# Layer 1 of a four-layer graph network: all turned parts of the factors prepared ahead of the loop, in the first product buffer of the round

## The chip, the cores and the metric

The kernel runs on one core of one Trainium2 chip. The metric is the device time of one execution in microseconds; for the kernel before, three executions took 556.18, 557.09 and 557.86 us, so the median is 557.09 us. The engines are named as in the profile: PE (TensorE), with PEld for its weight loads, DVE (VectorE), ACT (ScalarE), POOL (GpSimd) and SP (SyncE, which here issues DMAs).

## The reference

Four layers run one after the other on a graph of 3327 nodes with 64 features each and a dense matrix `adj` of 3327 x 3327. Each is `x = layernorm(x + layer(x, adj))`. The change lies in layer 1, a hyperbolic attention layer:

```python
x_tan = _logmap0(x, C)
left = x_tan @ att_W[:D] + att_b
right = x_tan @ att_W[D:]
adj_att = jax.nn.sigmoid(left + right.T) * adj
x_local = _logmap(x[:, None, :], x[None, :, :], C)
support_t = jnp.einsum('ij,ijd->id', adj_att, x_local)
return _proj(_expmap(x, support_t, C), C)
```

For every pair of nodes i and j a logarithmic map is needed, whose only part that belongs to the pair is a function of the product of the two nodes' vectors. All the rest splits into factors that belong to i alone or to j alone.

## The kernel before

The nodes are padded to 26 blocks of 128. Two blocks, number b and number b + 13, stand side by side in one tile of 128 partitions, 64 features each, so that a turned matrix (features in partitions, nodes in columns) has 13 blocks of 128 columns. `riT` is the turned factor of the nodes i; `ljT[0]` is that of the nodes j; `ljT[1]` is the same with its two halves of partitions exchanged. Where a part of `ljT[0]` is made, two DMAs from the one to the other tile, issued by SP (`change_over`), make the same part of `ljT[1]`.

The loop of layer 1 goes over 104 tiles. A tile t is one block j (128 rows) against 832 of the columns i: two pieces of 416, one in each half. Two tiles that follow each other share the block j and make a pair. For each tile there are these steps:

- `attention` (once a pair): ACT computes `sg`, the sigmoid, 1664 columns; POOL multiplies it by the adjacency `at`. SP loads `at` into one of four buffers (`load`, line 1058); the last four blocks are kept in SBUF (`kept`).
- `products`: PE makes `pq`, the products of the vectors, in PSUM (line 1103; each of the two matmuls of float32 counts as more than one instruction in the profile).
- `linear`: DVE makes `a` from `pq` and `sg` (line 1115), and then ACT squares `pq` in place (line 1116).
- `gather`: DVE makes `v` from the squared `pq` and `a` (line 1124), and PE multiplies it into the accumulator `acc` (line 1136).

A pass (`cp`) over all 26 blocks makes 52 tiles, with two accumulators; there are two passes. In the first pass ACT also makes the rows `xv` of a block to come, one for each pair (`rows_of_sums`, line 1230).

The products stand in three PSUM buffers of two banks each, from the pool `n1q`; a buffer is used again when its last reader is done, which for a product is `v`. [...] Ahead of the loop the same six banks belong to another pool, `n1p`, in which the first parts of the factors are made.

PE, ACT, DVE and POOL carry out their instructions in the order in which the code writes them (a manual schedule); only SP's order is left to the scheduler. So the order of the calls is the order of the engines. In the loop it is, for each t: `linear(t + 1)`, then `gather(t)`, which after `v` calls `products(t + 3)`, then the attention of a pair to come.

The factors are turned on PE, by transposes against `ident` into PSUM; a copy then brings them to SBUF. Only a part of it is done before the loop: `right` of blocks 9 to 12 and 5 to 8 (the latter called `seventh`), `turn` of blocks 0 to 7. Four parts are made in the loop (`later`): at t = 13 `right` of blocks 1 to 4 and `turn` of 8 to 11, at t = 25 `right` of block 0 and `turn` of 12. At these two tiles `prepare` takes a product buffer (`prep_t` in the profile) for the transposes, ACT copies them out (line 1214) in the next step, and `products(t + 3)` is called behind the gather instead of ahead of it:

```python
if extra:
    copies.extend(prepare(f"t{t}", extra))
if not extra:
    products(t + 3)
```

`by_rows` is a further part, the factor `lf` turned to 26 rows, made in the bank of the second accumulator; `spread_left` later stores it to DRAM and loads it back, spread over all partitions.

Of the kernel before, what the change touches and what calls it, by code (L numbers as in the profile page):

```python
# [10 lines left out]
F32 = mybir.dt.float32  # L11
# [8 lines left out]
P = 128  # L20
N = 3327
NB = 26
# [54 lines left out]
def kernel(  # L77
# [819 lines left out]
    with tc.tile_pool(name="l1", bufs=1) as l1:  # L897
# [20 lines left out]
        with tc.tile_pool(name="l1a", bufs=1) as l1a, tc.tile_pool(  # L918
            name="l1ap", bufs=1, space=PSUM
        ) as l1ap:  # L920
            v = l1a.tile([P, NB], F32, name="v")
            sums = l1a.tile([P, NB], F32, name="sums")
# [88 lines left out]
        def near_sphere(mT, ljT_0, xm, sq_e, t_e, rows_63):  # L1011
# [3 lines left out]
            with tc.tile_pool(name="n1", bufs=1, reuse_waits="tile") as n1, tc.tile_pool(  # L1015
# [45 lines left out]

                orders = (order, sorted(order, key=lambda jb: jb in kept))
                tiles = [(cp, jb, ci) for cp in range(2) for jb in orders[cp] for ci in range(2)]
                us, pqs, a_s, accs, copies, sums = {}, {}, {}, {}, [], []

                def attention(pair):

# [49 lines left out]
                        pqs[t], pqs[t], AF.Square, bias=al[:, one], scale=ga[:, one]  # L1117
                    )

                def gather(t, extra=()):  # L1120

                    cp, jb, ci = tiles[t]
                    w = n1w.tile(TW, F32, tag="v", name=f"v_{t}")
                    stt(w, pqs.pop(t), CUBIC_REST, a_s.pop(t), op0=ALU.add, op1=ALU.mult)  # L1124
                    while sums:
                        sums.pop(0)()
                    if extra:
                        copies.extend(prepare(f"t{t}", extra))
                    if not extra:
                        products(t + 3)  # L1130
                    if jb == orders[cp][0]:
                        accs[cp, ci] = n1c.tile(
                            [P, CW], F32, tag=f"acc{ci}", name=f"acc1_{cp}_{ci}"
                        )
                    for h in range(2):
                        nc.tensor.matmul(  # L1136
                            accs[cp, ci][h * D : (h + 1) * D, :], xv[:, slot(jb), :], w[:, h, :],
                            start=(jb == orders[cp][0]), stop=(jb == orders[cp][-1]),
                        )
                    if extra:  # L1140
                        products(t + 3)
                    if jb == orders[cp][-1]:
                        of = slice((2 * cp + ci) * CW, (2 * cp + ci + 1) * CW)
                        sums.append(lambda: nc.scalar.copy(mT[:, of], accs[cp, ci]))
                        if t + 1 == len(tiles):
                            while sums:
                                sums.pop(0)()
# [43 lines left out]
                def change_over(b, n):  # L1191
                    of = slice(b * P, (b + n) * P)
                    nc.sync.dma_start(ljT[1][D:, of], ljT[0][:D, of])
                    nc.sync.dma_start(ljT[1][:D, of], ljT[0][D:, of])
# [7 lines left out]
                        )  # L1202
                    return riT[:, b * P : (b + n) * P], pt[:, : n * P]

                def prepare(name, parts):

                    pt = n1q.tile([P, 2, 512], F32, tag="pq", name=f"prep_{name}")
                    return [made(pt[:, k], *part) for k, part in enumerate(parts)]

                def made(pt, make, b, n):  # L1210
                    dst, src = make(pt, b, n)

                    def copy(to=nc.scalar.copy):
                        to(dst, src)
                        if make is right and b < 9:
                            change_over(b, n)

                    return copy

# [14 lines left out]
                def bank(which, make, b, n):  # L1234

                    pt = n1c.tile([P, 4 * P], F32, tag=f"acc{which}", name=f"prep_{make.__name__}_{b}")
                    return made(pt, make, b, n)
# [3 lines left out]
                    pt = n1p.tile([P, 4 * P], F32, name=f"first_{make.__name__}_{b}")  # L1241
                    return made(pt, make, b, n)

                later = {13: ((right, 1, 4), (turn, 8, 4)), 25: ((right, 0, 1), (turn, 12, 1))}
                with tc.manual_schedule(
                    engines={
                        mybir.EngineType.PE, mybir.EngineType.Activation, mybir.EngineType.DVE,
# [49 lines left out]
                    n1q = pairs.enter_context(  # L1297
                        tc.tile_pool(name="n1q", bufs=3, space=PSUM, reuse_waits="tile")
                    )
                    by_rows = bank(1, left_rows, 0, NB)  # L1300
                    products(0)
                    products(1)
                    seventh = bank(0, right, 5, 4)
                    products(2)
                    list(attention(1))
                    rows_of_sums(order[0])
                    linear(0)
                    seventh()
                    list(attention(2))
                    for t in range(len(tiles)):  # L1310
                        linear(t + 1)
                        if t == 0:
                            by_rows()
                            rows_of_sums(order[1])
                        while copies:
                            copies.pop(0)()
                        gather(t, later.get(t, ()))
                        if t % 2 == 0:
                            list(attention(t // 2 + 3))
                            if t // 2 + 2 < NB:  # L1320
                                rows_of_sums(order[t // 2 + 2])
                        if t == 8:
                            spread_left(7)
                        if t == len(tiles) - 4:
                            of = slice(0, 2 * CW)
                            nc.gpsimd.tensor_tensor(xm[:, of], mT[:, of], ljT[0][:, of], ALU.mult)
                            gp = nc.gpsimd

                            gp.tensor_scalar(gs, g1, MIN_NORM, -256.0, ALU.max, ALU.mult)
                            gp.tensor_tensor(gk, gs, ga, ALU.mult)  # L1330
                            gp.tensor_scalar(gks, gk, -2.0, None, ALU.mult)
                            gp.tensor_tensor(gs2, gs, gs, ALU.mult)
                            gp.tensor_scalar(aav, aa, 1.0 / D, LN_EPS, ALU.mult, ALU.add)
                            gp.tensor_tensor(rows_63, but_last[:, :1], but_last[:, 1:], ALU.add)
                        if t == len(tiles) - 3:
                            pq = n1q.tile([P, 2, 512], F32, tag="pq", name="pq_early")
                            pm = pq[:, :, : 3 * (P + 2)].rearrange("p a (k w) -> p a k w", k=3)
                            for b in range(6):
                                nc.tensor.matmul(
                                    pm[:, b // 3, b % 3], mT[:, b * P : (b + 1) * P], all_m,  # L1340
                                    start=True, stop=True,
                                )
                        if t == len(tiles) - 2:
                            nc.scalar.activation(
                                sq_e.rearrange("p (a k h) d -> p a k (h d)", a=2, k=3),
                                pm[..., :P], AF.Square,
                            )
                            nc.scalar.copy(
                                t_e.rearrange("p (a k h) -> p a k h", a=2, k=3), pm[..., P:]
                            )  # L1350
# [521 lines left out]
```

## Time and profile before

| | |
|---|---|
| median of three runs | 557.09 us (556.18 to 557.86) |
| the profiled execution's own time | 557.54 us |
| its span | 555.7 us |
| loop of layer 1, first `a` to last `v` | 22.20 to 224.3 us |
| `a` of DVE (line 1115) | 104 of 1013 ns, 105.3 us busy |
| `v` of DVE (line 1124) | 104 of 1014 ns, 105.4 us busy |
| square of ACT (line 1116) | 104 of 1012 ns, 104.6 us busy |
| product with `at` on POOL (line 1088) | 44 of 3738 ns and 10 with `kept` |
| granted PE clock over the span | 0.979 |

An entry of the timeline gives the start in us, the time taken in us, engine, line, operation, output and inputs with their shapes, and in brackets how long the engine stood idle before it and what it waited for. Instructions of one engine overlap a little: an `a` of 1013 ns is followed by the next DVE instruction 0.93 us after its start. The profiled execution's time stands 0.45 us above the median.

### The profile page before, as it was taken

The numbers are of one execution on the slowest core, as the hardware profiler recorded it, in microseconds if no ns is written. First come the engines' busy times: TensorE is split into PE (matmuls) and PEld (weight loads), VectorE is DVE, ScalarE is ACT, GpSimd is POOL, SyncE is SP. The second block draws the span as 40 slices with busy tenths as digits, with TensorE's granted clock in tenths as the row PEclk, the third lists the DMA queues.
The fourth block names the chain that finished last, engine by engine and source line by source line (L and its number), as shares of the span: only waits on it lengthen the run. The fifth ranks groups of instructions, "written<-read, shape, count | busy, mean of one in ns | idle before, by whom it ended". The sixth has DMA issues, their size and how long they took to land.

```text
span 555.7 us, 7392 instructions
## 1 busy us (share of the span) xinstructions
PE 527.5 (95%) x2841; PEld 226.9 (41%) x2841; DVE 372.2 (67%) x549; ACT 276.8 (50%) x325; POOL 207.4 (37%) x85
## 2 busy tenths in 40 slices
PE   8799989999999999999999999999999999999991
PEld 5422222222222222964444444434455555545541
DVE  6799999999999999798000011200678877887733
ACT  4899999999999997620000100000464333433321
POOL 3699999999999999000000000000001000000000
PEclk9889999999999999799999999999999999999996
DMA  8958866666667536799998049999029994799601
GB/s 282 365 205 288 257 209 225 210 223 220 225 232 243 187 123 247 277 416 425 423 427 367 1 163 424 426 426 399 6 66 344 329 326 167 246 296 349 247 1 38
DMA packets 33893, 143.57 MB, mean 258 GB/s; under 512 B 10269, under 2 KB 11959, under 8 KB 28855
## 3 DMA queue, kind: packets, MB, share of 16 engines
q1 hardware_dynamic: 31511, 142.40, 69.7%
q10 hardware_dynamic: 2336, 0.59, 0.5%
q8 instruction: 24, 0.39, 0.3%
q14 instruction: 22, 0.18, 0.1%
HBM read 141.53 MB, written 0.87 MB: 256 GB/s over the span
## 4 chain that ended last, share of the span: by engine, by line
PE 68%; DVE 17%; issue 7%; ACT 6%; POOL 1%; DVEq 0%; POOLq 0%; ACTq 0%
PE cnt L421 26%; PE cnt L526 11%; DVE v L1124 10%; PE pq L1103 9%; PE acc L722 6%; PE acc L1136 4%; PE acc L737 3%; ACT pq L1116 3%; ACT sg L1076 2%; DVE a L1115 2%; DVE w L539 1%; PE cnt L412 1%; DVE mask L341 1%; PE idle L928 1%; PE x_w L1455 1%
## 5 line engine op out<-in xcount | busy, mean ns | idle before, releaser
L1088 POOL TENSOR_TENSOR sg<-sg,at 128x1664 f32<-128x1664 f32 x44 | 163.7, 3738 | 3.7 <-ACT sg L1076 2.2
L1103 PE MATMUL pq<-riT,ljT 64*128 64x416 f32 x416 | 101.0, 564 | 11.6 <-DVE v L1124 7.9
L1116 ACT ACTIVATE pq<-pq,al,ga 128x832 f32<-128x832 f32 x104 | 104.6, 1012 | 12.1 <-DVE a L1115 12.0
L1115 DVE SCALAR_TENSOR_TENSOR a<-pq,sg 128x832 f32<-128x832 f32 x104 | 105.3, 1013 | 4.5 <-PE pq L1103 2.3
L1124 DVE SCALAR_TENSOR_TENSOR v<-pq,a 128x832 f32<-128x832 f32 x104 | 105.4, 1014 | 3.3 <-ACT pq L1116 2.2
L1136 PE MATMUL acc<-v,xv 128*64 128x416 f32 x416 | 96.0, 541 | 0.0
L1076 ACT ACTIVATE sg<-lb,rb 128x1664 f32<-128x1664 f32 (+1 forms) x53 | 87.3, 1649 | 0.0
L541 ACT ACTIVATE w<-cnt 128x832 int16<-128x832 f32 x55 | 47.3, 863 | 71.5 <-PE cnt L526 71.4
L421 PE MATMUL cnt<-at_l,lj 128*64 128x416 f32 x448 | 80.4, 513 | 0.0
L653 POOL TENSOR_TENSOR s<-sq,s 128x384 bf16<-128x384 f32 (+1 forms) x4 | 4.1, 1026 | 200.7 <-ACT s L652 200.7
L506 ACT ACTIVATE x<-cnt 128x416 f32<-128x416 f32 x8 | 4.1, 518 | 131.5 <-PE cnt L421 131.5
L539 DVE TENSOR_SCALAR w<-cnt 128x832 int16<-128x832 f32 x49 | 50.1, 1023 | 25.8 <-PE cnt L526 24.0
L1103 PEld LDWEIGHTS pq<-riT,ljT 64*128 64x128 f32 x416 | 31.7, 186 | 85.1 <-DVE v L1124 78.6
L526 PE MATMUL cnt<-mask,tri 128*128 128x416 bf16 x208 | 53.5, 339 | 0.1
L722 PE MATMUL acc<-w,s 128*128 128x416 bf16 x208 | 52.6, 339 | 0.5 <-DVE hid L794 0.5
L526 PE MATMUL cnt<-mask,rest 128*128 128x416 bf16 x200 | 51.6, 340 | 1.2 <-ACT w L541 0.6
L421 PEld LDWEIGHTS cnt<-at_l,lj 128*64 128x64 f32 x448 | 31.9, 137 | 46.2 <-issue 45.4
L1136 PEld LDWEIGHTS acc<-v,xv 128*64 128x64 f32 x416 | 20.7, 135 | 61.5 <-issue 57.8
L409 DVE COPY lj<-pn_l 128x512 f32<-128x512 f32 (+1 forms) x4 | 2.4, 592 | 61.6 <-PE pn_l L373 61.6
L341 DVE TENSOR_SCALAR mask<-ah 128x1664 bf16<-128x1664 f32 x42 | 43.4, 1034 | 0.0
L421 PE MATMUL cnt<-kept,lj 128*64 128x416 f32 x224 | 41.2, 513 | 0.0
L586 DVE TENSOR_TENSOR x<-x,xc 128x416 f32<-128x416 f32 x4 | 2.4, 588 | 41.5 <-ACT x L506 41.5
(285 smaller groups left out, 441.9 us busy)
## 6 DMA issues: line engine op xcount, KB each, us to landing
at_l<-in_adjT SPq DMA_DIRECT2D x24, 1664.0 KB, 12.8
at<-in_adjT SPq DMA_DIRECT2D x44, 832.0 KB, 4.9
ah<-in_adjT SPq DMA_DIRECT2D x42, 832.0 KB, 6.3
bt_l<-in_adjT SPq DMA_DIRECT2D x8, 1664.0 KB, 14.9
kept<-in_adjT SPq DMA_DIRECT2D x7, 1664.0 KB, 8.1
lb<-lf_rows SPq DMA_DIRECT2D x2, 384.0 KB, 6.1
ljT<-ljT SPq DMA_DIRECT2D x4, 128.0 KB, 5.5
x<-in_x ACTq DMA_DIRECT2D x1, 416.0 KB, 5.4
```

The lines of the kernel that those rows point to most:

```text
L341: nc.vector.tensor_scalar(mask[q], at, 0.0, None, ALU.not_equal)
L421: nc.tensor.matmul(acc[c][h * D : (h + 1) * D, :], hw[:, slot(jb), :], blocks[jb][:, o : o + CW], start=c not in begun, stop=last, skip_gr ...
L526: nc.tensor.matmul(cnt[c][:, e, :], mat, mask[q][:, of], start=start, stop=(mat is tri), skip_group_check=True,)
L539: nc.vector.tensor_scalar(w.bitcast(I16), cnt[c], 0.0, None, ALU.max)
L722: nc.tensor.matmul(acc[h, c][:, e, :], s12[:, slot(jb)].rearrange("p t d -> p (t d)"), ws[q, c][:, e, :], start=first, stop=last,)
L1076: nc.scalar.activation(sg[:, :, of], lbs[:, :, of], AF.Sigmoid, bias=rb[:, sl : sl + 1])
L1088: nc.gpsimd.tensor_tensor(sg[:, :, of], sg[:, :, of], at[:, :, of], ALU.mult)
L1103: nc.tensor.matmul(pq[:, h, :], ljT[h != jb // NBH][rows, of], riT[rows, ch * CW : (ch + 1) * CW], start=True, stop=True,)
L1115: stt(a_s[t], pqs[t], CUBIC_PLUS, us.pop(t), op0=ALU.add, op1=ALU.mult)
L1116: nc.scalar.activation(pqs[t], pqs[t], AF.Square, bias=al[:, one], scale=ga[:, one])
L1124: stt(w, pqs.pop(t), CUBIC_REST, a_s.pop(t), op0=ALU.add, op1=ALU.mult)
L1136: nc.tensor.matmul(accs[cp, ci][h * D : (h + 1) * D, :], xv[:, slot(jb), :], w[:, h, :], start=(jb == orders[cp][0]), stop=(jb == orders[c ...
```

## The change

All four parts that were made in the loop are now made ahead of it.

- `by_rows` and the two single blocks (`right` of 0, `turn` of 12) share one bank, `prep_few`, that of the second accumulator.
- The two parts of four blocks (`right` of 1 to 4, `turn` of 8 to 11) share one product buffer, `prep_fours`, which is the first that the pool of products gives out. The third product, `products(2)`, gets this buffer next, and so is called after both parts have been copied out.
- The four copies are made by DVE (`copy` is its tensor copy) instead of ACT: three ahead of the first `a` (`linear(0)`), one between it and the second `a`.
- The exchange of halves (`change_over`) for `right` of 1 to 4 and of 0 is not called with the copy but later, at t = 4 and t = 10 (`changes`).
- `gather` always calls `products(t + 3)` ahead of the accumulation; `prepare`, `copies`, `later` and `extra` are gone.

```diff
-                def gather(t, extra=()):
+                def gather(t):
...
-                    if extra:
-                        copies.extend(prepare(f"t{t}", extra))
-                    if not extra:
-                        products(t + 3)
+                    products(t + 3)
...
-                    if extra:
-                        products(t + 3)
...
-                def prepare(name, parts):
-
-                    pt = n1q.tile([P, 2, 512], F32, tag="pq", name=f"prep_{name}")
-                    return [made(pt[:, k], *part) for k, part in enumerate(parts)]
-
-                def made(pt, make, b, n):
+                def made(pt, make, b, n, at_once=True):
                     dst, src = make(pt, b, n)
 
                     def copy(to=nc.scalar.copy):
                         to(dst, src)
                         if make is right and b < 9:
-                            change_over(b, n)
+                            if at_once:
+                                change_over(b, n)
+                            else:
+                                changes.append((b, n))
...
-                later = {13: ((right, 1, 4), (turn, 8, 4)), 25: ((right, 0, 1), (turn, 12, 1))}
...
-                    by_rows = bank(1, left_rows, 0, NB)
+                    few = n1c.tile([P, 4 * P], F32, tag="acc1", name="prep_few")
+                    by_rows = made(few[:, :P], left_rows, 0, NB)
+                    singles = [
+                        made(few[:, k * P : (k + 1) * P], make, b, 1, False)
+                        for k, make, b in ((1, right, 0), (2, turn, 12))
+                    ]
+
+                    fours_of = n1q.tile([P, 2, 512], F32, tag="pq", name="prep_fours")
+                    rows_1 = made(fours_of[:, 0], right, 1, 4, False)
                     products(0)
+                    rows_1(copy)
+                    for part in singles:
+                        part(copy)
+                    rows_8 = made(fours_of[:, 1], turn, 8, 4)
                     products(1)
                     seventh = bank(0, right, 5, 4)
-                    products(2)
                     list(attention(1))
                     rows_of_sums(order[0])
                     linear(0)
+                    rows_8(copy)
+                    products(2)
                     seventh()
                     list(attention(2))
                     for t in range(len(tiles)):
...
-                        while copies:
-                            copies.pop(0)()
-                        gather(t, later.get(t, ()))
+                        gather(t)
...
+                        if t in (4, 10):
+                            change_over(*changes.pop(0))
```

In the built program's order this moves two things more. On SP, the two DMAs that exchange blocks 1 to 4 stand between the loads of `at` for blocks 11 and 10, and those of block 0 between the two loads of `lb` and the load for block 20; before, they stood further back, after the copies at t = 14 and t = 26. On PE, the transposes of `turn` 8 to 11 stand between the first and the second product.

More of the change, by code (lines that the diff above doesn't have):

```diff
@@ L1063, in near_sphere @@
                 tiles = [(cp, jb, ci) for cp in range(2) for jb in orders[cp] for ci in range(2)]
-                us, pqs, a_s, accs, copies, sums = {}, {}, {}, {}, [], []
+                us, pqs, a_s, accs, changes, sums = {}, {}, {}, {}, [], []
                 def attention(pair):
```

## The prediction

> **What bounds the kernel now.** I read the page first: its part 2 shows TensorE near 9 everywhere, and VectorE, ScalarE and GpSimd at 9 only in the first sixteen slices, which are layer 1. The change touches nothing else, so the question is what sets the pace of that loop (20 to 224 us). The table by stretches answers it (columns: stretch, then busy us and instruction count of PE, PEld, DVE, ACT, POOL; then clock, DMA share, GB/s).
>
> ```profile
> 46.91:54.56 7.65, 7.38 (x36) 2.55 (x36) 7.55 (x9) 7.49 (x10) 7.65 (x3) 1.00 0.83 274
> 54.56:71.14 16.58, 15.47 (x70) 4.29 (x68) 15.17 (x17) 15.88 (x19) 16.00 (x5) 1.00 0.79 232
> 71.14:78.79 7.65, 6.74 (x30) 1.89 (x30) 7.55 (x9) 7.49 (x10) 7.47 (x3) 1.00 0.67 212
> ...
> 133.69:215.64 81.95, 79.91 (x352) 21.95 (x352) 81.95 (x89) 77.27 (x66) 81.95 (x23) 1.00 0.63 210
> ```
>
> The reader is to see that in the last stretch DVE has no idle time at all, and that before it DVE, ACT and POOL are all within a few per cent of full. POOL is the engine one could take for the bound. The waits tell otherwise.
>
> ```profile
> DVE a L1115 <- PE pq L1103: 2.3, 2, 1.2
> DVE v L1124 <- ACT pq L1116: 2.2, 5, 1.2
> DVE a L1115 <- POOL sg L1088: 2.1, 2, 1.3
> ```
>
> DVE waited for POOL in two places only, both at the start (22.20 and 24.11 us below). Twice, 1.15 us each, it waited for a product. The timeline shows the first of these:
>
> ```profile
> 52.63 0.42 PEld L1175 LDWEIGHTS prep_t<-ident,lj 128*128 128x128 f32 x4 [0.77 <-DVE v L1124]
> ...
> 53.61 1.02 DVE L1124 SCALAR_TENSOR_TENSOR v<-pq,a 128x832 f32<-128x832 f32 x1
> ...
> 54.69 1.89 PE L1103 MATMUL pq<-riT,ljT 64*128 64x416 f32 x8
> 54.96 0.59 ACT L1214 COPY riT<-prep_t 128x512 f32<-128x512 f32 x1
> ...
> 55.78 1.02 DVE L1115 SCALAR_TENSOR_TENSOR a<-pq,sg 128x832 f32<-128x832 f32 x1 [1.15 <-PE pq L1103]
> ```
>
> At tile 13 prep_t takes the product buffer that v of tile 13 has just freed (52.63, where every other tile has its product). The product of tile 16 must wait for v of tile 14 (53.61) to free the next (54.69), and DVE, in order, stands until it is there (55.78). Tile 25 repeats it with two small transposes: what costs is the buffer's turn, not the size. What it does to the pace I read from the starts of a in the VectorE timeline, four tiles apart: tiles 4, 8, 12: 31.61, 39.26, 46.91 (7.65 each); 16: 55.78 (8.87); 20, 24: 63.50, 71.14 (7.72, 7.64); 28: 80.00 (8.86); 32, 36: 87.71, 95.35 (7.71, 7.64). So the pace is 7.65 before, between and after, and each preparation adds 1.22 and 1.21, with 0.07 and 0.06 in the four tiles behind it.
>
> The other place is the start, where the work would go:
>
> ```profile
> 20.25 0.69 DVE L1214 COPY riT<-first_turn 128x512 f32<-128x512 f32 x1 [0.33 <-PE first_turn L1199]
> ...
> 22.20 1.02 DVE L1115 SCALAR_TENSOR_TENSOR a<-pq,sg 128x832 f32<-128x832 f32 x1 [1.26 <-POOL sg L1088]
> ...
> 23.32 1.02 ACT L1116 ACTIVATE pq<-pq,al,ga 128x832 f32<-128x832 f32 x1 [0.38 <-DVE a L1115]
> 24.11 1.02 DVE L1115 SCALAR_TENSOR_TENSOR a<-pq,sg 128x832 f32<-128x832 f32 x1 [0.89 <-POOL sg L1088]
> 24.27 0.59 ACT L1214 COPY ljT<-prep_right 128x512 f32<-128x512 f32 x1
> ...
> 26.21 0.97 PE L1103 MATMUL pq<-riT,ljT 64*128 64x416 f32 x4 [2.75 <-DVE v L1124]
> ```
>
> DVE is idle for 1.26 us before the first a and 0.89 before the second, because POOL has not finished sg; PE is idle for 2.75 us up to 26.21.
>
> [...]
>
> **The change part by part.**
> 1. Removed from the loop: two turns of a product buffer. DVE gets back 1.22 + 1.21 + 0.07 + 0.06 = 2.56 us. What is late next? ScalarE's rhythm, which makes the pace 7.65 rather than the 7.45 of four tiles after 133.69; it is in force on both sides of each stall, so I let it stay. POOL would have to keep up: it runs back to back at about 3.70 us a pair from 35.23 to 61.09, 7.40 per four tiles. It ends pair 3 at 35.2 and a of tile 6 starts at 35.34; pair 4 ends at 38.9 and a of tile 8 starts at 39.26, and from there its lead grows by 0.25 per four tiles. Its waits in the loop (1.14 us at 85.67, 0.37 at 61.46) end 0.08 after ScalarE's sigmoids, so they follow the stalls and go with them. At the end it finishes at 217.5 and its a starts at 219.37: 1.9 us to spare. POOL's whole waiting, 3.7 us, is more than is taken out, so it doesn't become the bound.
> 2. ScalarE loses four copies (0.59, 0.59, 0.27, 0.27 us) at 54.5 and 78.7. They lie in the stalls; counted there already.
> 3. PE at the start: two single transposes and two fours, ten in all, of 0.13 us spacing (four first_turn in 0.66 us, of which 0.27 is one alone). In order: by_rows at 20.05 (prep_left_rows in the trace of before, so placed there), singles to 20.44, the four of right to 20.96 with the last landing at about 21.1; pq_0 to 21.9; four of turn to 22.4; pq_1 to 23.3; the seventh's four to 23.8, landing 24.0. ScalarE wants the last at 24.27: hidden by 0.2.
> 4. DVE at the start: copy of 512 columns from 21.15, next start 0.6 later at 21.75, then two of 128 columns at about 0.2 spacing (the 128x128 product at 238.77 is followed at 238.97[...]): a_0 may start at 22.15[...], against POOL's 22.20. Then a_0, and the copy of rows_8 (0.6) from 23.13 to 23.75, in the gap before 24.11. Cover: POOL's first two halves of sg. If it were gone, 1.0 + 0.6 = 1.6 us would be on the chain, since the chain of waits runs POOL, a_0, square, ScalarE there. I take 0.1 us, range 0 to 0.5.
> 5. The third product now waits for the copy of rows_8: ready at 23.8, so PE runs it at 24.1 to 25.1, inside PE's gap of 2.75; behind it wait pq_3 and the first gather, which wait for v_0 at 26.06 anyway. Cost nothing; with the gap filled, the half clock at 28 to 31 may vanish or move. It costs little now, since POOL ends pair 2 at 31.56 and a of tile 4 starts at 31.61. Bounds: 0 and 0.3 gained.
> 6. SP's queue: the build's order puts the two crossing DMAs of blocks 1 to 4 between the loads at_0_11 and at_0_10, and the two of block 0 ahead of at_0_20, instead of at 58.03 and 81.13. Four issues of about 0.6 us. at_0_10 moves from about 27 to 28.5 and is needed at 42.6; the pair of block 0 fits between 40.8 and at_0_20's 42.69, which itself waits for POOL and is needed near 53.7 after 4.9 us of flight: 6.1 us to spare. Cost nothing. The crossed blocks are first read by products after 80 us.
>
> Sum: 2.56 − 0.1 = about 2.45 us; I call it 2.4. The profiled execution took 557.54 us (span 555.7 and 1.84 around it), so 555.1 by that one; it lies 0.45 above the median of 557.09, and I forecast against the median: 554.7. Later layers start on events of the loop's end (the loads of layer 2 wait for its buffers, PE for lj), so they move as a whole.
>
> **The rivals.** About 0.3%, 1.7 us, is what a measurement of this kernel tells from no change.
> - POOL sets the pace. For it: busy all of 133.69 to 215.64. Against: DVE never waits for it there. It then gains only what POOL waited at the stalls, 0.37 + 1.14 = 1.5: 555.6.
> - The start gives back. Three copies and ten transposes in a stretch where POOL, DVE and ScalarE hand over without slack. At 0.5 to 1.6 us of loss, say 1.0: 555.7.
> - Slower: the half clock. Place: tiles 1 to 5.[...] At half clock a product takes 1.76 instead of 0.97 us and a gather 1.41 instead of 0.92 (both at 28 to 31.6), so a tile costs 1.3 us more than its cadence of 1.9 can hide. Two tiles cancel the gain; four would give 557.1 + 5.2 − 2.4 = 559.9. For it: the trace has such a window just there. Against: the change shortens the gap that precedes it, and before, it lasted 3 us and cost nothing past POOL.
> - That the change doesn't do what it says: the built order shows the ten transposes ahead and none in the loop, so no.
>
> **How the numbers follow.** As reasoned 0.76 (554.7; its own range 554.1 to 555.3), POOL's pace 0.07, the start 0.08, half clock or another loss 0.09. The two middle ones fall within 0.3%, so faster 0.76, same 0.15, slower 0.09. The range runs from 553.8 (0.3 of clock gained, and the runs' scatter of about 0.6 around their median) to 556.3, which takes in both middle cases.
>
> **What would show it.** Right: no DVE wait for a product at tiles 16 and 28; starts of a 7.65 apart from tile 8 to 48; the loop's last v near 220.9 instead of 223.32; a_0 still at 22.2 and waiting for POOL. Wrong: a_0 later than 22.5 (step 4); POOL's end in front of a by nothing (step 1); clock 0.50 over more than 3 us (the slower case); an SP issue after 48.8 for at_0_20 (step 6).

## The result and the profile after

| | before | after |
|---|---|---|
| median of 20 executions each, us | 557.24 | 555.40 |
| ratio of the times, 95% interval | | 0.9975 [0.9964, 0.9986] |
| profiled execution: time (span), us | 557.54 (555.7) | 555.63 (553.8) |
| a of tile 0 starts | 22.20 | 24.54 |
| a of tile 8 | 39.26 | 41.40 |
| from tile 8 to tile 48 | 79.03 | 76.42 |
| a of tile 100 | 215.64 | 215.18 |
| from there to the end of the span | 340.1 | 338.6 |

The ratio is a gain of 1.4 us (0.8 to 2.0); the forecast was 2.4. The medians alone differ by 1.84 us, the means (557.17 and 555.72 us) by 1.45; below, a gain is always the one of the ratio. The two profiled executions differ by 1.9, but the lower half of the table shows that this 1.9 isn't the change at work: the loop got 2.6 shorter, the start 2.1 longer, and 1.4 came from behind tile 100, where the program is the same.

The loop first. The stretches of the trace after, cut at the starts of a of tiles 12, 16, 24, 28 and then over the eleven last fours (columns as before: busy us and count of PE, PEld, DVE, ACT, POOL; clock, DMA share, GB/s):

```profile
49.04:56.68 7.64, 7.27 (x32) 1.99 (x32) 7.54 (x9) 7.48 (x10) 7.64 (x3) 1.00 0.79 259
56.68:71.97 15.29, 14.54 (x64) 3.99 (x64) 15.10 (x18) 14.98 (x18) 14.98 (x5) 1.00 0.72 231
71.97:79.61 7.64, 7.27 (x32) 1.99 (x32) 7.54 (x9) 7.49 (x10) 7.46 (x3) 1.00 0.67 214
133.23:215.18 81.95, 79.89 (x352) 21.94 (x352) 81.95 (x89) 77.27 (x66) 81.95 (x23) 1.00 0.63 210
```

Four tiles take 7.64 us at the places of the two old stalls (first and third line) and between them, and the last stretch takes 81.95 as it did. ScalarE's rhythm stayed the pace, as forecast: once in four tiles v starts just behind ScalarE's square (48.10 and 55.74 us). POOL, though busy for all of the first line, didn't become the bound (point 1 of the part on the prediction). The waits of DVE between 20 and 225 us (total, times, longest):

```profile
DVE v L1124 <- ACT pq L1116: 2.5, 4, 1.2
DVE riT L1204 <- PE first_turn L1194: 2.1, 1, 2.1
DVE a L1115 <- PE prep_fours L1194: 0.5, 1, 0.5
```

The two waits of a for a product in the loop are gone, and so are both waits of a for POOL, which had stood at the start. In their place DVE waits 2.1 us for transposes, before the first a. The timeline of the start shows it:

```profile
20.42 1.95 POOL L1088 TENSOR_TENSOR sg<-sg,kept 128x832 f32<-128x832 f32 x1
...
21.50 0.66 PE L1194 MATMUL first_turn<-ident,mT 128*128 128x128 f32 x4
...
22.19 0.69 DVE L1204 COPY riT<-first_turn 128x512 f32<-128x512 f32 x1 [2.06 <-PE first_turn L1194]
...
22.95 0.69 DVE L1204 COPY ljT<-prep_fours 128x512 f32<-128x512 f32 x1
23.00 0.33 PEld L1103 LDWEIGHTS pq<-riT,ljT 64*128 64x128 f32 x4 [0.32 <-issue]
23.03 0.97 PE L1103 MATMUL pq<-riT,ljT 64*128 64x416 f32 x4
...
23.76 0.28 DVE L1204 COPY riT<-prep_few 128x128 f32<-128x128 f32 x1
...
24.54 1.02 DVE L1115 SCALAR_TENSOR_TENSOR a<-pq,sg 128x832 f32<-128x832 f32 x1 [0.50 <-PE prep_fours L1194]
```

Before, POOL's first half of `sg` released a (that half alone took 1.96 us, to 22.17, and a started at 22.20):

```profile
20.21 7.69 POOL L1088 TENSOR_TENSOR sg<-sg,kept 128x832 f32<-128x832 f32 x4
```

After, that half ends at 20.42 + 1.95 = 22.37, and a starts 2.17 later. Two things added up. The last transposes of `first_turn` are late: they land only now, at 22.19 instead of 20.25. And behind their copy stand the new copies and a later product. Why the transposes are late is in the stretches of one microsecond (the sixth value behind the length is the clock):

```profile
19.00:20.00 1.00, 1.00 (x8) 0.67 (x8) 1.00 (x2) 1.00 (x3) 0.00 (x0) 0.50 1.06 453
20.00:21.00 1.00, 1.00 (x14) 1.00 (x12) 0.13 (x1) 0.34 (x1) 0.72 (x2) 0.50 1.04 439
21.00:22.00 1.00, 1.00 (x11) 0.70 (x8) 0.00 (x0) 0.39 (x1) 1.00 (x1) 0.80 0.99 416
```

The same in the trace of before:

```profile
19.00:20.00 1.00, 1.00 (x16) 0.83 (x13) 0.92 (x2) 1.00 (x3) 0.00 (x0) 1.00 1.00 426
20.00:21.00 1.00, 1.00 (x7) 0.34 (x7) 0.69 (x1) 1.00 (x2) 0.94 (x2) 1.00 1.03 429
```

After, PE ran at half clock from 14.6 to 21.4 us, where in the trace of before it was full again from 17.5. Four transposes of `first_turn` took 1.06 us at half clock (from 18.64) and 0.66 at full (from 21.50). All of that lies ahead of the first instruction that the change adds. So three explanations stood open: the start of the changed kernel costs something of its own (theory A), or nothing (B), or what is missing is scatter of the clock (C).

The end of the two traces shows such a scatter. One microsecond in layer 2, in the trace of before:

```profile
234.00:235.00 1.00, 1.00 (x7) 1.00 (x7) 1.00 (x12) 0.99 (x4) 0.00 (x0) 0.50 1.00 426
```

and in the trace of after:

```profile
234.00:235.00 1.00, 1.00 (x11) 1.00 (x11) 0.67 (x5) 0.49 (x2) 0.00 (x0) 1.00 1.00 426
```

Before, the clock was halved there from 229.1 to 236.0, after only from 229.6 to 233.0. That goes with the 1.4 us behind tile 100, and it isn't the change's: a second trace of the kernel before (below) has 338.8 us behind tile 100, and a variant of the changed kernel (the single copies behind, below) has 340.1. In the 14 traces of this case, the two with 6.8 us of half clock there have 340.1, and the twelve with 3.4 us or none have 338.4 to 339.2.

### The profile page after: what moved, and what is told of

It is laid out like the page before. It is cut to its first block, busy times and chain, and to the rows that moved or that the text cites. A ratio compares the mean times of both kernels' runs of the same rounds, so it can differ in the third digit from the quotient of the medians.

```text
span 553.8 us, 7395 instructions
## 1 busy us (share of the span) xinstructions
PE 526.6 (95%) x2841; PEld 226.3 (41%) x2841; DVE 373.4 (67%) x553; ACT 275.5 (50%) x321; POOL 207.6 (37%) x85
## 4 chain that ended last, share of the span: by engine, by line
PE 64%; DVE 17%; ACT 10%; issue 7%; DVEq 0%; POOL 0%; ACTq 0%; POOLq 0%
PE cnt L421 26%; PE cnt L526 11%; DVE v L1124 10%; PE pq L1103 6%; PE acc L722 6%; ACT pq L1116 4%; ACT sg L1076 4%; PE acc L737 3%; PE acc L1133 2%; DVE a L1115 2%; DVE w L539 1%; PE cnt L412 1%; DVE mask L341 1%; PE idle L928 1%; PE pm L1416 1%
## 5 line engine op out<-in xcount | busy, mean ns | idle before, releaser
L1088 POOL TENSOR_TENSOR sg<-sg,kept 128x1664 f32<-128x1664 f32 (+1 forms) x10 | 30.0, 3023 | 0.8 <-ACT sg L1076 0.8
## 6 DMA issues: line engine op xcount, KB each, us to landing
at_l<-in_adjT SPq DMA_DIRECT2D x24, 1664.0 KB, 12.1
bt_l<-in_adjT SPq DMA_DIRECT2D x8, 1664.0 KB, 16.8
```

The costliest lines, as they stand in the source:

```text
L1088: nc.gpsimd.tensor_tensor(sg[:, :, of], sg[:, :, of], at[:, :, of], ALU.mult)
```

## The experiments

### The loop alone, the start alone, and another order

The first takes the four preparations out of the loop without putting them anywhere: DMAs fill these parts of the factors with other columns instead.

```diff
-                later = {13: ((right, 1, 4), (turn, 8, 4)), 25: ((right, 0, 1), (turn, 12, 1))}
+                later = {}
...
+                        if t == 4:
+                            nc.sync.dma_start(riT[:, 8 * P :], ljT[0][:, 5 * P : 10 * P])
+                            nc.sync.dma_start(ljT[0][:, : 5 * P], ljT[0][:, 5 * P : 10 * P])
+                            change_over(0, 5)
```

> The kernel before without the four parts made in the loop: riT of blocks 8 to 12 and ljT of blocks 0 to 4 are filled by DMA with other turned columns, so those factors have wrong values; nothing is added to the start of PE, DVE or ScalarE. Theory A (the loop gives the forecast 2.56 us, and the added work at the start costs about 1 us on average, because it is exposed when the PE clock is halved there): 2.3 to 2.7 us below before, that is about 1 us below the changed kernel. Theory B (the start is free, and the loop gives only what was measured): 1.2 to 1.8 us below before, as the changed kernel. Starts of a: 7.65 us per four tiles from tile 8 to tile 48 under both in a profile.

Measured: 0.9957 [0.9942, 0.9972], that is 2.4 us gained (1.6 to 3.2); a of tile 8 at 39.13, 76.43 us from tile 8 to 48. So the loop gives what was forecast for it: 2.6 us in the trace, and the time agrees.

The second is the changed kernel with the four preparations made once more in the loop, as before (without their DMAs).

```diff
+                    later = {13: ((right, 1, 4), (turn, 8, 4)), 25: ((right, 0, 1), (turn, 12, 1))}
...
+                        while copies:
+                            copies.pop(0)()
-                        gather(t)
+                        gather(t, later.get(t, ()))
```

> The changed kernel's start, with the four parts made a second time in the loop as before. Theory A: 0.6 to 1.5 us above before, since only the price of the start is left. Theory B: within 0.3 us of before. In the profile the steps of 8.87 at tiles 16 and 28 are back under both; the first a says whether the copies stood ahead of it.

Measured: 0.9999 [0.9988, 1.0009]. In its trace both stalls are back (79.01 us from tile 8 to 48) and a of tile 8 stands at 40.14, 0.88 later than before. The trace speaks for theory A; the time, whose interval ends at +0.5 us, only allows a price of up to that, less than the 0.6 to 1.5 that theory A expected. This run alone didn't decide.

The third keeps everything of the change but the order: the first two products go ahead of the two fours, which take the third product buffer; their copies follow a of tile 0, and the two single copies follow a of tile 1.

```diff
-                    fours_of = n1q.tile([P, 2, 512], F32, tag="pq", name="prep_fours")
-                    rows_1 = made(fours_of[:, 0], right, 1, 4, False)
                     products(0)
-                    rows_1(copy)
-                    for part in singles:
-                        part(copy)
-                    rows_8 = made(fours_of[:, 1], turn, 8, 4)
                     products(1)
                     seventh = bank(0, right, 5, 4)
+                    fours_of = n1q.tile([P, 2, 512], F32, tag="pq", name="prep_fours")
+                    rows_1 = made(fours_of[:, 0], right, 1, 4, False)
+                    rows_8 = made(fours_of[:, 1], turn, 8, 4)
                     list(attention(1))
                     rows_of_sums(order[0])
                     linear(0)
+                    rows_1(copy)
                     rows_8(copy)
                     products(2)
...
                         if t == 0:
                             by_rows()
                             rows_of_sums(order[1])
+                            for part in singles:
+                                part(copy)
```

> The changed kernel with prep_fours in the third buffer of the round instead of the first: PE makes pq_0 and pq_1 first, and all four copies stand behind a_0 (two between a_0 and a_1, two between a_1 and v_0). Theory A: nothing stands ahead of a_0, so most of the start's price goes: 0.5 to 1.2 us below the changed kernel, about 2.3 below before. Theory B: as the changed kernel within 0.3 us, or slower if the copies push v_0 and v_1 back.

> The changed kernel again, as the others' neighbour on the same chip. Theory C (the missing microsecond is scatter): about 2.4 below before. Theories A and B: 1.2 to 1.8 below. Its profile shows whether the PE clock is halved between 18 and 22 us again, and where a_0 starts if it isn't: at full clock theory A expects a_0 at about 22.2, right when POOL's first half of sg is done.

Measured: 0.9962 [0.9947, 0.9977] for the other order, with a of tile 0 at 22.13 and waiting for POOL, and of tile 8 at 39.20; 0.9962 [0.9944, 0.998] for the changed kernel once more, with a of tile 0 at 23.46 and of tile 8 at 40.32. In this second trace the clock was full from 18.9 on, and the start was still 0.7 us late against POOL. So the price isn't only what happens while the clock is halved: at full clock from 18.9 on, theory A expected a of tile 0 at 22.2. The times of these two runs decide nothing. Both gain 2.1 us: for the changed kernel that is nearer to theory C's 2.4 than to the 1.2 to 1.8 of A and B, and the other order isn't the 0.5 to 1.2 us faster that A expected.

### What a of tile 0 waits for

The next four: the kernel before again, for a second trace; two variants of the changed kernel, each with one step moved; and the other order again. The first variant tests theory A1, that a of tile 0 waits for the four `turn` transposes that the trace names:

```diff
-                    rows_8 = made(fours_of[:, 1], turn, 8, 4)
                     products(1)
+                    rows_8 = made(fours_of[:, 1], turn, 8, 4)
```

The second moves the two single copies behind a of tile 2:

```diff
-                    for part in singles:
-                        part(copy)
...
+                        if t == 1:
+                            for part in singles:
+                                part(copy)
                         gather(t)
```

> The kernel before, once more, for a second trace of it. Theory A (the start of the changed kernel costs 0.7 to 1 us by its order of work, clock or no clock): a of tile 0 again 2.0 us after POOL's first sg and a of tile 8 19.05 us after it; the granted clock plays no part. Theory D (the longer stretch at half clock, up to 18.5 to 21.6 us in all three traces with the changed start against 17 in three without, belongs to the change): half clock ends at about 17 and comes back at 27 to 31. Theory C (the clock is a lottery that has nothing to do with the change): any pattern, and the time at half clock near 230 us may be 3.4 or 6.8 us long.

> The changed kernel with the four turn transposes for blocks 8 to 11 moved behind the second product. Theory A1 (a of tile 0 waits 0.49 us for these transposes, as the trace names them): a of tile 0 starts 0.4 to 0.5 us earlier, 2.4 to 2.5 us after POOL's first sg instead of 2.9, and DVE's wait before it shrinks to under 0.15; a of tile 8 comes 19.3 to 19.4 us after POOL's first sg instead of 19.8; the time 0.4 us less than the changed kernel's. Rival A2 (it waits for the product itself, which ends later than the trace models it): a of tile 0 stays 1.5 us after the start of its product, and the time doesn't move.

> The changed kernel with the two 128-column copies moved from ahead of a of tile 0 to behind a of tile 2. Theory A1 (a waits for the transposes, and these for the first 512-column copy and for PE's queue): a of tile 0 doesn't move, since the copies end 0.49 us before it; DVE's idle time before it grows by 0.4 to 0.9 us. The rival of the prediction's step 4 (the copies themselves make a late): a of tile 0 starts 0.4 us earlier, the time falls by 0.4 us.

> The version with the two fours in the third product buffer, behind the first two products, once more. Theory A: a of tile 8 19.05 us after POOL's first sg, the loop from tile 8 to 48 in 76.4 us, 554.3 to 555.0 by mean, 0.5 to 1 us below the changed kernel. Theory B/C (the start is free, the rest is scatter): no different from the changed kernel's pooled 555.4.

The timeline of the kernel before, second trace (one execution, 557.71 us):

```profile
20.64 1.95 POOL L1088 TENSOR_TENSOR sg<-sg,kept 128x832 f32<-128x832 f32 x1
...
22.48 0.69 DVE L1214 COPY riT<-first_turn 128x512 f32<-128x512 f32 x1 [2.12 <-PE first_turn L1199]
...
22.52 1.68 PE L1103 MATMUL pq<-riT,ljT 64*128 64x416 f32 x8
...
23.63 1.02 DVE L1115 SCALAR_TENSOR_TENSOR a<-pq,sg 128x832 f32<-128x832 f32 x1 [0.46 <-PE pq L1103]
```

This was the key reading. The unchanged kernel had the long half clock too, up to 21.8 us, and its a of tile 0 then came 1.4 us later than in the trace on which the prediction rests, waiting for a product and not for POOL; a of tile 8 at 40.79. Theory D, that the long half clock belongs to the change, falls. So does the form of theory A in which the clock plays no part: it expected a 2.0 us after POOL's first `sg`, and it came 2.99 after. And it shows that two chains run to the first a: POOL's, and that of the last `first_turn` copy.

The timeline with the turn transposes behind the second product (0.9961 [0.9944, 0.9978]):

```profile
20.23 0.69 DVE L1204 COPY riT<-first_turn 128x512 f32<-128x512 f32 x1 [0.21 <-PE first_turn L1194]
...
20.31 11.39 POOL L1088 TENSOR_TENSOR sg<-sg,kept 128x832 f32<-128x832 f32 x5
...
21.07 1.67 PE L1103 MATMUL pq<-riT,ljT 64*128 64x416 f32 x8
...
21.80 0.28 DVE L1204 COPY riT<-prep_few 128x128 f32<-128x128 f32 x1
22.57 1.02 DVE L1115 SCALAR_TENSOR_TENSOR a<-pq,sg 128x832 f32<-128x832 f32 x1 [0.49 <-POOL sg L1088]
22.67 0.66 PE L1194 MATMUL prep_fours<-ident,mT 128*128 128x128 f32 x4
```

The transposes now run behind a, and a still starts 1.50 us after its product begins and 0.49 after the last copy, as in the changed kernel (24.54 against 23.03 and 23.76 + 0.28). So they weren't what a waited for, although the trace named them: theory A1, which expected the wait to shrink to under 0.15, falls. A wait is put down to whatever ended last just before it, and here the name merely changed to POOL, whose half had ended 0.31 earlier (20.31 + 1.95 = 22.26). With the single copies behind a (0.9966 [0.9955, 0.9978]):

```profile
20.30 11.39 POOL L1088 TENSOR_TENSOR sg<-sg,kept 128x832 f32<-128x832 f32 x5
...
21.05 0.69 DVE L1204 COPY riT<-first_turn 128x512 f32<-128x512 f32 x1 [1.03 <-PE first_turn L1194]
...
21.89 0.97 PE L1103 MATMUL pq<-riT,ljT 64*128 64x416 f32 x4
...
22.97 1.02 DVE L1115 SCALAR_TENSOR_TENSOR a<-pq,sg 128x832 f32<-128x832 f32 x1 [0.47 <-PE pq L1103]
```

Now a starts 1.08 us after its product, as in the kernel before (23.63 against 22.52: 1.11). The rival named in that expectation holds: the two copies ahead of a make it 0.42 later (the times, 0.9966 against 0.9975 and 0.9962, are too coarse to show it). The rest of the delay is PE's: from the start of the last `first_turn` copy to the first product it is 0.84 us here and in the changed kernel (23.03 - 22.19), and 0.04 in the kernel before, so 0.80 more. Some 0.6 of it are the six new transposes in front of the product: with the two single ones alone in front it is 0.22 (next timeline), and the four follow each other at 0.11 us. The other 0.2 is a turn of buffers. The pool hands out its three product buffers in turn. In the built program the first, which `prep_fours` takes, lies in the banks of `first_right` and of a `first_left`, long free; the second, which is now the first product's, lies in those of `first_wrong` and of the last `first_turn`. So the first product has to wait for the end of that copy, as before only the second one did. In the timeline of after, the copy ends at 22.19 + 0.69 = 22.88 and the product starts 0.15 later, 0.35 after the weights of the transposes; where nothing held a product up behind four transposes, that pause was 0.17 (24.51 in the same trace). In the other order (0.9957 [0.9938, 0.9976]), where the first product has the first buffer back and only the two singles in front of it, most of this is undone. (Theory A expected a of tile 8 at 19.05 behind POOL here; it was 19.49, as the copy began 1.03 behind POOL.)

```profile
20.09 11.48 POOL L1088 TENSOR_TENSOR sg<-sg,kept 128x832 f32<-128x832 f32 x5
...
21.12 0.69 DVE L1204 COPY riT<-first_turn 128x512 f32<-128x512 f32 x1 [1.32 <-PE first_turn L1194]
...
21.34 1.67 PE L1103 MATMUL pq<-riT,ljT 64*128 64x416 f32 x8
...
22.43 1.02 DVE L1115 SCALAR_TENSOR_TENSOR a<-pq,sg 128x832 f32<-128x832 f32 x1 [0.61 <-PE pq L1103]
```

At a of tile 0 copies, transposes and buffer together make 1.20 us behind the `first_turn` copy (24.54 - 22.19 = 2.35, against 23.63 - 22.48 = 1.15 before). Some 0.3 of it is made up before tile 8, where 0.9 is left.

### Two chains, and a clock that decides between them

From here a theory E, with one rule for all traces: a of tile 8 starts at the later of two times, POOL's first `sg` plus 19.05 us, and the last `first_turn` copy plus 18.3 us (before) or 19.2 us (after). The three numbers were read from the traces so far; the four that follow were forecast with them. The change adds 0.9 us to the second chain alone. In the ten traces so far the copy began 0.57 us or more behind POOL where PE's half clock ended at 18.9 us or later, and at most 0.04 behind where it ended by 17.5. To try whether PE's work ahead of it moves that end, as the author supposed, the matmuls of line 986, which only keep PE busy, were taken out of both kernels, or made wider and more:

```diff
-                if i in (0, 3):
-                    w = 2 if i else 4
-                    nc.tensor.matmul(
-                        idle[:, : w * P], ident, center_4[:, :w], start=True, stop=True
-                    )
```

and, for the other pair, instead of these lines:

```diff
+                if i in (0, 1, 2, 3):
+                    nc.tensor.matmul(idle, ident, center_4, start=True, stop=True)
```

> The kernel before without the idle matmuls of line 986[...]. Theory E (the start is the later of two chains: POOL's first sg plus 19.05 us, which the change leaves as it is, and the last first_turn copy plus 18.3 us, which the change lengthens to 19.2; the half clock delays the second alone): half clock to 19 us or later, the last first_turn copy 1 us or more behind POOL's first sg, a of tile 8 at that copy plus 18.3 us. Rival C (scatter): a of tile 8 follows POOL by 19.05 whatever the clock.

> The changed kernel without the same idle matmuls. Theory E: a of tile 8 at the last first_turn copy plus 19.2 us, so the pair without idle matmuls differs by only 2.6 - 0.9 = 1.7 us. Rival: it differs as the other pairs do.

> The kernel before with idle matmuls of full width behind each of the first four groups of line 980[...]. Theory E: full clock from 17 us or earlier, the last first_turn copy no later than POOL's first sg, a of tile 8 at POOL's first sg plus 19.05 us.

> The changed kernel with the same added idle matmuls. Theory E: a of tile 8 at the later of POOL's first sg plus 19.05 us and the last first_turn copy plus 19.2 us, at most 0.2 us more than the kernel before from POOL; the pair differs by 2.4 to 2.6 us, more than the pair without idle matmuls by about 0.7. Rival: both pairs differ by the same.

Without the idle matmuls, the kernel before:

```profile
20.18 1.95 POOL L1083 TENSOR_TENSOR sg<-sg,kept 128x832 f32<-128x832 f32 x1
21.40 0.69 DVE L1209 COPY riT<-first_turn 128x512 f32<-128x512 f32 x1 [1.51 <-PE first_turn L1194]
...
39.74 1.01 DVE L1110 SCALAR_TENSOR_TENSOR a<-pq,sg 128x832 f32<-128x832 f32 x1
```

and the changed one:

```profile
19.96 1.96 POOL L1083 TENSOR_TENSOR sg<-sg,kept 128x832 f32<-128x832 f32 x1
21.37 0.69 DVE L1199 COPY riT<-first_turn 128x512 f32<-128x512 f32 x1 [1.70 <-PE first_turn L1189]
...
40.57 1.01 DVE L1110 SCALAR_TENSOR_TENSOR a<-pq,sg 128x832 f32<-128x832 f32 x1
```

The last lines are a of tile 8: 18.34 and 19.20 us behind the `first_turn` copy, as the rule says. With more idle matmuls, the changed kernel:

```profile
22.42 0.68 DVE L1201 COPY riT<-first_turn 128x512 f32<-128x512 f32 x1
22.79 15.07 POOL L1085 TENSOR_TENSOR sg<-sg,kept 128x832 f32<-128x832 f32 x6
...
41.85 1.01 DVE L1112 SCALAR_TENSOR_TENSOR a<-pq,sg 128x832 f32<-128x832 f32 x1
```

Here POOL is the later one, and a of tile 8 follows it by 19.06: behind POOL the start costs nothing. The added matmuls delayed both chains, though, POOL's to 21.82 us in the kernel before and to 22.79 in the changed one. All traces by the rule (times in us; "half" is the stretch at half clock before 25 us):

| kernel | half | POOL's first sg | last first_turn copy | a of tile 8 | behind POOL | behind the copy |
|---|---|---|---|---|---|---|
| before | 14.1 to 17.5 | 20.21 | 20.25 | 39.26 | 19.05 | 19.01 |
| before, again | 15.0 to 21.8 | 20.64 | 22.48 | 40.79 | 20.15 | 18.31 |
| before, fewer idle | 13.1 to 20.0 | 20.18 | 21.40 | 39.74 | 19.57 | 18.34 |
| before, more idle | none | 21.82 | 21.45 | 41.10 | 19.28 | 19.65 |
| loop alone | 13.0 to 16.5 | 20.08 | 19.71 | 39.13 | 19.04 | 19.42 |
| after | 14.6 to 21.4 | 20.42 | 22.19 | 41.40 | 20.98 | 19.21 |
| after, again | 12.1 to 18.9 | 20.55 | 21.12 | 40.32 | 19.78 | 19.21 |
| start alone | 12.2 to 19.0 | 20.11 | 20.94 | 40.14 | 20.02 | 19.19 |
| turns behind | 14.0 to 17.4 | 20.31 | 20.23 | 39.44 | 19.13 | 19.21 |
| after, fewer idle | 13.3 to 20.1 | 19.96 | 21.37 | 40.57 | 20.61 | 19.20 |
| after, more idle | 13.7 to 17.1 | 22.79 | 22.42 | 41.85 | 19.06 | 19.43 |
| singles behind | 12.2 to 19.0 | 20.30 | 21.05 | 39.83 | 19.53 | 18.79 |
| other order | 13.3 to 16.8 | 20.14 | 19.83 | 39.20 | 19.07 | 19.38 |
| other order, again | 12.7 to 19.5 | 20.09 | 21.12 | 39.58 | 19.49 | 18.46 |

Where the change's start is in it, a of tile 8 is never less than 19.19 behind the copy, and never under 19.05 behind POOL. The one line 0.2 off the rule is "before, more idle", where the clock was halved from 27.1 to 33.9 us, in tiles 2 to 4. (At the end of the table, "singles behind" and "other order" start differently.) The gap between the chains goes with the end of the half clock: where it ended at 17.5 us or earlier, or didn't come, the copy began from 0.37 ahead of POOL to 0.04 behind; where it ended between 18.9 and 21.8, from 0.57 to 1.84 behind.

How long it lasted goes with where it began, and not with the kernel. With line 986 as it was it lasted 3.4 us in the four traces where it began between 13.0 and 14.1 us, and 6.8 in the six where it began at 12.1 to 12.7 or at 14.6 to 15.0; the old and the new start are in both groups. Without the idle matmuls it lasted 6.8 from 13.1 and from 13.3; with more of them it didn't come before 25 us in one trace and lasted 3.4 from 13.7 in the other. This pattern was seen afterwards and not tested, and two traces of each don't show that the idle matmuls move the half clock.

The single copies account for 0.42 of the 0.9 (19.21 to 18.79), the four `right` transposes and the buffer for most of the rest (18.46 in the other order, 18.31 to 18.34 before).

The times agree, less sharply. With fewer idle matmuls 0.9997 [0.9983, 1.001] and 0.9968 [0.9954, 0.9983]: the pair differs by 0.0029, 1.6 us, where 1.7 was expected. With more, 1.0034 [1.0021, 1.0046] and 0.9984 [0.9974, 0.9993]: 0.0050, 2.8 us, where 2.4 to 2.6 was expected. That the second pair differs by more than the first, as expected, isn't shown. The times don't tell it from nothing; in the traces a of tile 8 is 0.83 us later in the first pair and 0.75 in the second, there because POOL's own first `sg` came 0.97 later, and why it did is open. What the traces show is which chain a of tile 8 follows, and at which distance.

## Why the prediction was right, and what was mis-sized

The direction and the mechanism of the loop were right; the sum was too large by the term of the start. The median, 555.40 us, lies within the range of 553.8 to 556.3, but just outside the 554.1 to 555.3 that the prediction gave its own sum: the range held it because it was drawn wide enough for the rivals. The gain of 1.4 us is also below the 1.7 that the prediction called the least that can be told from no change, though its interval excludes none, and nearer to its rival "the start gives back" (555.7) than to its sum (554.7). Of its signs, the even pace and the missing waits for a product came. The loop's last v stood at 222.87 instead of near 220.9, and the sign against step 4, a_0 later than 22.5, came too (24.54). The clock was at 0.50 for more than 3 us, but ahead of the loop and not where the slower case had it.

1. The loop, 2.56 us: measured 2.61 (79.03 to 76.42), and from 2.58 to 2.61 in every pair of traces. That the pace of 7.65 is ScalarE's and stays, that POOL keeps up and is 1.9 us ahead at the end (its last `sg` ends at 217.06, and a of tile 102, which needs it, starts at 218.91): as stated. The rival "POOL sets the pace", which left 1.5 of it, falls.
2. The four copies that ScalarE lost lay in the stalls: nothing beyond point 1 was gained.
3. PE at the start. The seventh's transposes delayed nothing, as forecast: in the second trace of the changed kernel they land at 25.0 and ScalarE takes them at 25.53. The first product was forecast to be done at 21.9; at the clock of the trace of before (turns behind) it began at 21.07, and one product took 0.97 (24.25 in that trace). The step counted its transposes but not that it changes buffers, and so waits for the last `first_turn` copy (0.2 us).
4. DVE at the start, "I take 0.1 us, range 0 to 0.5", an estimate of the author's: this is the term that was mis-sized. At the clock of the trace it was read from, it is nearly right: with the half clock ending at 17.4 (turns behind) a of tile 8 came 0.18 later than before, 0.08 of it against POOL (a of tile 0 came 0.37 later, at 22.57, as it started 0.49 and not 0.2 behind the last copy). But the 0.1 compares the copies' end with POOL's end in a trace where both chains began within 0.04 us of each other (20.21 and 20.25), as if that were fixed. In ten traces with line 986 as it was, the copy chain began from 0.37 us ahead of POOL to 1.84 behind it; all of that lies ahead of what the change adds. With the rule above, each of the ten gives a price for the change, 19.2 plus that gap, less the later of 18.3 plus the gap and 19.05, and nothing below zero: 0.9 in five of them, 0.7 in one, and from 0 to 0.2 in four, on average 0.55. The gain is then 2.61 - 0.55 = 2.06 us, an estimate; measured were 1.4 (0.8 to 2.0) and, again, 2.1 (1.1 to 3.1). The prediction saw the case ("if it were gone, 1.0 + 0.6 = 1.6 us would be on the chain") and gave it, as the rival "the start gives back", a chance of 0.08. It isn't a case with a chance: it is what happens in six traces of ten.
5. The half clock at 28 to 31 us (granted clock 0.50 in each of these microseconds in the trace of before, behind PE's gap of 2.75), "may vanish or move": it is in all five traces with the start of before (between 26.7 and 33.9 us), in none of the seven with the changed start or with the singles behind, and in one of the two with the other order. As forecast its going gained nothing that shows, since POOL leads there; only where it lasted twice as long (before, more idle) were 0.2 us lost. What the prediction took as one place was two: the same event ahead of the loop, between 12.1 and 21.8 us, is the one that matters. It was in the trace of before too (14.1 to 17.5), and the prediction drew on the loop's part alone. Its place changed from trace to trace: where it came it began between 12.1 and 15.0 us and lasted 3.4 or 6.8 us.
6. SP's queue: the load behind the two exchanges of block 0 was issued at 43.75 us, and no wait in the loop is for a load. Cost nothing, as forecast.

The forecast slower case, the half clock in tiles 1 to 5, a supposition of the author's, occurred in no trace of the changed kernel. Open: the start alone should by the rule be 0.55 us slower than before; it measured between 0.7 us faster and 0.5 slower, and 0.55 is just outside.

Better than both? The other order has the start of before and the loop of after, so by the rule it gains up to 0.7 us more than the changed kernel where the half clock is long, and nothing where it is short. Its two measurements (0.9962 and 0.9957) and the changed kernel's (0.9975 and 0.9962) lean that way, but their intervals overlap. It is the better start by the traces and not shown faster by the times. Four of the 22 executions of its first measurement took 557.5 to 559.3 us, at granted clocks of 0.973 to 0.975, the lowest of all here; the other 18 took 553.5 to 556.0. None of the four was traced, so what this order risks is open.

## What to carry to other kernels

When work is moved into the start, list every chain that runs to the first step of the loop and how far apart they are, and price the move against the one that it lengthens; "hidden by 0.05 us" in one trace is no cover, and a second trace of the unchanged kernel (here the fifth experiment) tells how far that gap wanders. Compare two profiles by stages before comparing their spans: here 1.4 of 1.9 us came from unchanged code. And when the trace names who ended a wait, move that one instruction: if the wait stays, it was something else.

## What the runs showed that was not expected

- The half clock at 28 us in the trace of before came behind a gap of PE of 2.75 us (up to 26.21), but the one at 14.1 came although PE was shown as busy: from 10.7 to 14.1 PE has no gap of more than 0.22 us, and 1.95 us of it are sixteen matmuls of 128x4. What brings the half clock wasn't tried by itself.
- In the traces with both single copies right ahead of a of tile 0 and no other release in sight, a started 0.49 us after the last copy's end (24.04 to 24.54, and 22.08 to 22.57, where POOL's half had ended at 22.26 and the first product lay between 21.07 and 22.04). With more idle matmuls it was 0.34 (24.55 to 24.89), and the end of POOL's half, at 24.74, lay between the two. Behind one copy of 512 columns it starts without such a pause (24.05 + 0.68 to 24.64 in the other order). Why is open.
- A 128x128 copy of DVE out of PSUM took 0.28 us, and the next instruction started 0.20 us after its start (23.56 and 23.76). The prediction took about 0.2 from another 128x128 operation, and that holds; the trace of before has such a copy too, in a later layer (line 409 at 326.53), and it took 0.29.
- Half clock for 6.8 instead of 3.4 us just behind the loop went with 1.4 us more in the first two traces, as much as the change itself. Between 3.4 us of it and none no difference shows.
